# A list kernel for a two-layer graph network: one gather table per group instead of one for all, the last group's lists in buffers of their own, a changed planner, and ScalarE taking part in layer 1's sorting while layer 0 runs

## The chip, the cores and the metric

The kernel runs on one core of a Trainium2 chip. The metric is the device time of one execution in microseconds (us); the kernel before takes 1524.7 us in the median of three runs (1523.92 to 1529.08). The engines are called by the profile's names: PE (matrix products), DVE (VectorE), ACT (ScalarE), POOL (GpSimd) and SP, whose queue issues most plain DMAs. POOL issues the indirect DMAs (gathers and scatters whose rows are named by an index per partition).

## The reference

There are 16 graphs of 1024 nodes with 64 channels; `adj` (16 x 1024 x 1024, float32, 64 MB) holds edge weights and is sparse: a graph's first node is expected to have some 60 neighbours, most nodes fewer than 10.

```python
# layer 0
h = jnp.maximum(_layernorm(x), 0.0)
x = x + matmul(adj / clip(sum(adj, 2), 1), h)
# layer 1
h = jnp.maximum(_layernorm(x), 0.0)
adj_d = _dilate_adj(adj, mask)                       # drops every skip-th neighbour of long lists
agg = _weighted_nanquantile_agg(h, adj_d > 0)        # per channel: 0.25, 0.5 and 0.75 quantiles
out = h + agg                                        # over a node's neighbours, weights .25 .5 .25
y = relu(out @ W1 + b1) @ W2 + b2
x = x + y * mask
```

A quantile over the neighbours needs each node's neighbour rows sorted, channel by channel. That is the costly part.

## The kernel before, in words

The work is one program with two layers that overlap.

**Layer 0** goes batch by batch (one graph is a batch). SP loads eight adjacency row tiles of 128 x 1024 (`at`, 512 KB each, five buffers; `loads`). ACT makes signs of them with row sums (`sg`, `signs`); DVE multiplies the signs by a key and takes the eight largest of each of four segments (`rec`, the neighbour list of each node; `listing`, L598). PE transposes each tile into `pt` and ACT copies that to `att` (`transposes`, `turned`, L628); PE multiplies `att` with the normed `h` (`products`, L659); DVE adds the residual into `row`. `channels` (L704) norms the result, and SP writes it as 66 values a node to a DRAM table, `tab`, of which each batch has 1025 rows (the last holds "no neighbour"). `endings` (L716) puts the batch's nodes in order of their degree class: ACT writes the lists into `row`, DVE works out each node's place (`to`), and POOL sends the rows to `srt[g]` by eight scatters `srt<-row,to`.

**Layer 1** goes by groups of four batches. `group(g)` (L1069) starts when its four batches are done and, from the third group on, when all ten jobs of group g - 2 are done; it loads `recs` from `srt[g]`, takes the neighbours' numbers out of the lists (`keys`), makes row numbers (`idx`, `nodes_i`), and enters into the table which neighbours the dilation drops, by two scatters `tab<-drop,didx` (L1166). It then makes ten jobs, one for each cap on the list length (15, 10, 8, and so on down to 1; the nodes in order of length lie in 32 tiles of 128, tile 0 holds those of the long lists, and tiles of one cap make one job). `recs`, `keys`, `idx` and `nodes_i` have two buffers for four groups.

A `Job` (L800) asks for one gather per place of its lists: `places<-tab,idx` brings 128 rows of 66 values to 128 partitions (496 gathers over the kernel). `Job.sort` (L850) works out on DVE which neighbours are dropped (`rem`, `gone`, `ok`) and the quantile weights (`w`), masks dropped values with a huge number, runs a sorting network of minima and maxima on DVE between `places` and `other`, and multiplies the sorted values by the weights. The mask and the products can be done by ACT, one instruction of 128 x 64 for each place ("helped", L882 and L965: `places<-places,gone` and `prod<-places,w`), or by DVE, one or a few instructions for all of it. In the kernel before ACT does so once all 16 batches of layer 0 are done. `layers` (L1007) sums on PE (`pt<-ident,prod`), runs the MLP over ACT and PE, DVE makes `y`, and POOL scatters it to the output (`out_dram<-y,nodes_i`).

**The long lists.** `long_lists` (L1188) serves the 32 longest nodes of each graph, eight of each per list: four lists of 88, 31, 24 and 20 gathers. For each it gathers the nodes' adjacency rows (`lat`), takes the neighbours by repeated maxima, and makes a job with `lplaces0` (the list of 88, one buffer) or `lplaces` (the others, two buffers, L1269). These read the table of all 16 batches; DVE's first step of such a sort is `lrem<-lplaces,lS`, its weights are `lw`. It is added after layer 0, in a pool of its own that takes the room of layer 0's buffers, so its first DVE instruction (`rev`) stands behind them.

**The order.** DVE's and POOL's orders are written into the program (`manual_schedule`, L357); the other engines' follow the Tile scheduler. What writes them is `Plan` (L232). Each piece of work is a generator that yields the engine of its next step and the time from which that step can begin; `run` takes the step that can begin first, ties by rank. `note` keeps a clock per engine with costs for every operation, the time `ready` of each tile, and the time `used`. The clocks are the planner's own, and only set the order. The run takes the groups first (rank -2000), then layer 0's streams in the ranks at L1278 to L1283, then `long_lists`.

All recorded operations have the line L226, that of the helper that notes them.

Of the kernel before, what the change touches and what calls it, by code (L numbers as in the profile page):

```python
# [9 lines left out]
F32 = mybir.dt.float32  # L10
BF = mybir.dt.bfloat16
# [16 lines left out]
GB = 4  # L28
SUB = 32
# [4 lines left out]

CAPS = (
    [0, 15, 10, 8, 7, 7, 6] + [5] * 4 + [4] * 4 + [3] * 6 + [2] * 6 + [1] * 5
)
LONG = (88, 31, 24, 20)
# [193 lines left out]
class Plan:  # L232
# [4 lines left out]
    def __init__(self, nc):  # L237
# [7 lines left out]
        self.last = self.own = None  # L245

# [21 lines left out]
    def note(self, engine, op, args, kwargs):  # L268
# [12 lines left out]
        after = 0.15  # L281
        if engine == "DVE":
# [9 lines left out]
        elif engine == "POOL":  # L292
            time, after = (1.27, 2.2) if op == "indirect_dma_start" else (0.15, 0.1)
            self.last = None
        else:
            start = max(start, self.clock["DMA"])
            rate = 165e3 if 4 * out.shape[-1] >= 512 else 85e3
            time, after = 0.05, 2.2 + math.prod(out.shape) * 4 / rate
            self.clock["DMA"] = start + after - 2.2
        self.clock[engine] = end = start + time  # L300
        self.ready[out.tensor.name] = end + after
# [64 lines left out]
def list_path(ctx, tc, x, adj, nodemask, w1, b1, w2, b2, out, go):  # L366
# [7 lines left out]
    NG = B // GB  # L374
# [7 lines left out]
    NTAU = N // SUB  # L382
# [45 lines left out]
    which = consts.tile([P, 2], I32, name="which")  # L428
    nc.vector.tensor_scalar(which[:, 1:2], part, 3, None, op0=OP.logical_shift_right)
    nc.vector.tensor_scalar(which[:, 0:1], which[:, 1:2], GB - 1, None, op0=OP.bitwise_and)  # L430
    toff = consts.tile([P, 2], F32, name="toff")
    nc.vector.tensor_scalar(toff, which, float(TS), None, op0=OP.mult)
    noff = consts.tile([P, 2], F32, name="noff")
    nc.vector.tensor_scalar(noff, which, float(N), None, op0=OP.mult)
    caps = consts.tile([P, NTAU], F32, name="caps")
    for t, cap in enumerate(CAPS):
        nc.vector.memset(caps[:, t:t + 1], float(cap if t else N))
# [28 lines left out]
    tab = dram.tile([B * TS, W], F32, name="tab")  # L466
    srt = [dram.tile([GB * N, RW], F32, name=f"srt{g}") for g in range(NG)]
# [3 lines left out]
    nc.sync.dma_start(tab.rearrange("(b t) w -> b t w", t=TS)[:, N, :], none)  # L471
    pairs = tab.rearrange("r (a two) -> (r a) two", two=2)
# [5 lines left out]
    plan = Plan(nc)  # L478
    nc = plan.nc
# [224 lines left out]
    def channels(pool, now):  # L704

        for b, st in enumerate(batch):
# [3 lines left out]
            yield from normed(row()[:, :, :C], row()[:, :, X1:R0])  # L710
            nc.sync.dma_start(
                tab[b * TS:b * TS + N, :].rearrange("(t p) w -> p t w", p=P), row()[:, :, :W]
# [3 lines left out]
    def endings(pool, now):  # L716

        first = lambda rank: rank - 3000
        for b, st in enumerate(batch):
            now[0] = b  # L720
            g, gb = divmod(b, GB)
# [20 lines left out]
            for s in STEPS[1:]:  # L742
# [26 lines left out]
            nc.vector.tensor_scalar(low, low, LSUB - 1, None, op0=OP.bitwise_and)  # L769
            nc.vector.tensor_scalar(  # L770
                pos, pos, float(GB), float(LSUB * gb), op0=OP.mult, op1=OP.add
            )
            to = new(pool, [P, NT], I32, "to", 2)
            nc.vector.scalar_tensor_tensor(to, low, float(1 - GB), pos, op0=OP.mult, op1=OP.add)
# [26 lines left out]
    class Job:  # L801
# [3 lines left out]
        def __init__(self, pool, n, T, keys, idx, node, mask, nodes_i, table, S, g, name="places",  # L805
                     bufs=4, rank=0):
# [3 lines left out]
        def run(self):  # L810
# [6 lines left out]
                at(self.idx), room(self.name, self.bufs), room("S", 4) if short else 0.0  # L817
# [8 lines left out]
            for t in range(T):  # L826
                for k in range(n - 1):
                    if t or k:
                        yield "POOL", pace, *own
                    since.append(since[0] if since else plan.clock["POOL"])  # L830
                    gather(A[:, k + 1, t, :], self.table, self.idx[:, t, k:k + 1])
                    progress["ahead"] -= 1
# [17 lines left out]
        def sort(self):  # L850
# [31 lines left out]
            helped = progress["batches"] == B  # L882
# [82 lines left out]
            helped = progress["batches"] == B  # L965
# [41 lines left out]
        def layers(self, terms, sources):  # L1007
# [55 lines left out]
            for t in range(T):  # L1063
                yield "POOL", lambda: at(y) + LATE
                scatter(out_rows, y[:, t, :], self.nodes_i[:, t:t + 1], scatters)
# [3 lines left out]
    def group(g):  # L1069


        yield "SP", lambda: 0.0 if progress["batches"] >= (g + 1) * GB and (
            g < 2 or progress["jobs"][g - 2] == len(set(CAPS[1:]))
        ) else INF
        R = (g + 1) * GB
        table = tab[:R * TS, :]
        recs = new(grp, [P, NTAU, REC], F32, "recs", 2)
# [8 lines left out]
            nodes, node, noff[:, 0:1], float(g * GB * N), op0=OP.add, op1=OP.add  # L1086
        )
        nodes_i = new(grp, [P, NTAU], I32, "nodes_i", 2)
# [491 lines left out]
```

## Time and profile before

| | |
|---|---|
| median of three runs | 1524.7 us |
| profiled execution, its own time | 1525.97 us |
| its span | 1523.8 us |
| mean granted PE clock | 0.689 |
| DVE busy | 1211.9 us, 80% |
| POOL busy | 960.8 us, 63% |
| ACT busy | 752.9 us, 49% |
| PE busy | 751.5 us, 49% |
| last `to` of layer 0 (DVE) ends | 772.1 us |
| last `srt` scatter (POOL) ends | 791.8 us |
| first step of the first long list's sort (DVE) | 1087.6 us |
| last output scatter starts | 1515.2 us |

Busy time is the time of the instructions themselves. The time in which an engine issues a DMA or waits for a semaphore isn't in it; "idle" lines of a group say what ended that time ("issue" where nothing shown did). A group's line gives operation, output <- inputs, form, count | busy time, mean of one in ns | idle time just before them and what ended most of it. The windows view gives busy time and number of instructions of each engine between two moments.

### The profile page before, as it was taken

Reading aid. Unit: us, or ns where it says so; the run is one execution under the profiler, and the core shown is the slowest. Engines: PE = TensorE matmul, PEld = TensorE weight load, DVE = VectorE, ACT = ScalarE, POOL = GpSimd, SP = SyncE. Lnnn points to the kernel's source line nnn. Section 1 sums busy time; section 2 is a strip of 40 time slices with the busy share of each in tenths; the row PEclk is TensorE's granted clock in tenths of the full one; section 3 lists DMA queues with packets and bytes.
Section 4 is the critical chain, followed back from the end, with each engine's and each line's share of the span. In section 5 each row is a group of like instructions: output and inputs, shape, how many; then the busy total and the mean of one; then the engine's idle time right before and its main releaser. Section 6 shows DMA issues by size and latency. Waiting matters only on the chain. (4 is left out here: it accounts for less than half of the span.)

```text
span 1523.8 us, 15747 instructions
## 1 busy us (share of the span) xinstructions
PE 751.5 (49%) x3192; PEld 469.3 (31%) x3192; DVE 1211.9 (80%) x4119; ACT 752.9 (49%) x2503; POOL 960.8 (63%) x1156
## 2 busy tenths in 40 slices
PE   4887776576348777655825420013000056706454
PEld 2443342344214453432413320012000034605343
DVE  6878798999997699999734779995189999998852
ACT  7989878476436665675515320011410147516442
POOL 0122237745567766556677776567777777777774
PEclk8889987787568778767865655555555556857666
DMA  4555764455514354643322131221111111112110
GB/s 153 172 163 156 185 187 116 131 134 172 113 40 104 114 144 129 161 131 83 87 52 37 29 78 34 50 41 31 33 23 24 26 27 30 37 30 45 36 27 17
DMA packets 135536, 129.01 MB, mean 85 GB/s; under 512 B 100696, under 2 KB 103384, under 8 KB 135432
## 3 DMA queue, kind: packets, MB, share of 16 engines
q1 hardware_dynamic: 102696, 86.46, 20.6%
q0 software_dynamic: 32736, 41.47, 12.6%
q14 instruction: 76, 0.62, 0.1%
q8 instruction: 28, 0.46, 0.1%
HBM read 108.57 MB, written 19.28 MB: 84 GB/s over the span
## 5 line engine op out<-in xcount | busy, mean ns | idle before, releaser
L226 POOL DMA_INDIRECT places<-tab,idx x496 | 495.0, 998 | 161.2 <-issue 142.3
L226 PE MATMUL pt<-ident,prod 128*128 128x128 f32 (+1 forms) x736 | 159.1, 376 | 454.0 <-DVE prod L226 369.6
L226 PEld LDWEIGHTS pt<-ident,prod 128*128 128x128 f32 (+1 forms) x736 | 129.4, 257 | 486.1 <-ACT prod L226 287.8
L226 PE MATMUL ps_small<-att,h 128*65 128x512 f32 x512 | 255.4, 649 | 26.9 <-ACT h L226 22.4
L226 POOL DMA_INDIRECT srt<-row,to x128 | 129.6, 1013 | 208.8 <-ACT row L226 186.7
L226 PE MATMUL pt<-ident,at 128*128 128x128 f32 x1024 | 181.0, 324 | 106.7 <-ACT att L226 79.2
L226 POOL DMA_INDIRECT lplaces<-tab,lidx x163 | 166.9, 1024 | 53.7 <-issue 49.1
L226 PEld LDWEIGHTS pt<-ident,at 128*128 128x128 f32 x1024 | 138.5, 166 | 154.2 <-ACT att L226 104.8
L226 DVE MAX8 rec<-sg 128x8 f16<-128x256 f16 x512 | 180.1, 414 | 4.4
L226 ACT ACTIVATE sg<-at 128x1024 f16<-128x1024 f32 x128 | 135.1, 1056 | 69.4 <-DMA at<-in_adj_dram 48.8
L226 ACT COPY att<-pt 128x512 f32<-128x512 f32 x256 | 141.4, 583 | 28.4 <-PE pt L226 27.3
L226 POOL DMA_INDIRECT out_dram<-y,nodes_i x124 | 121.8, 983 | 37.9 <-issue 20.0
L226 PEld LDWEIGHTS ps_small<-att,h 128*65 128x65 f32 x512 | 75.7, 153 | 166.8 <-issue 127.6
L226 ACT ACTIVATE gone<-gone 128x18 f32<-128x18 f32 (+9 forms) x23 | 4.8, 208 | 234.1 <-DVE ok L226 234.1
L226 DVE TENSOR_TENSOR sg<-sg,keyed 128x1024 f16<-128x1024 f16 x128 | 87.4, 683 | 30.4 <-ACT sg L226 30.4
L226 DVE TENSOR_TENSOR long_other<-lplaces 128x512 f32<-128x512 f32 (+5 forms) x124 | 63.8, 557 | 21.8 <-ACT lplaces L226 21.6
L226 PE MATMUL ps_small<-ot,w_sb 128*128 128x128 f32 (+3 forms) x112 | 53.1, 564 | 53.3 <-ACT ot L226 22.5
L226 ACT COPY ot<-pt 128x128 f32<-128x128 f32 (+3 forms) x56 | 22.2, 396 | 109.6 <-PE pt L226 109.3
L226 DVE TENSOR_TENSOR other<-places,other 128x64 f32<-128x64 f32 (+6 forms) x204 | 69.6, 341 | 5.9
L226 ACT ACTIVATE places<-places,gone 128x64 f32<-128x64 f32 x283 | 70.7, 335 | 0.4
L226 ACT ACTIVATE prod<-places,w 128x64 f32<-128x64 f32 x157 | 39.5, 335 | 63.1 <-DVE w L226 63.1
L226 DVE TENSOR_TENSOR places<-places,other 128x64 f32<-128x64 f32 (+2 forms) x208 | 62.4, 310 | 4.9
(210 smaller groups left out, 1643.3 us busy)
## 6 DMA issues: line engine op xcount, KB each, us to landing
at<-in_adj_dram SPq DMA_DIRECT2D x128, 512.0 KB
places<-tab,idx POOLq DMA_INDIRECT x496, 2.5
tab<-row SPq DMA_DIRECT2D x16, 264.0 KB
xt<-in_x_dram SPq DMA_DIRECT2D x16, 256.0 KB
lplaces<-tab,lidx POOLq DMA_INDIRECT x163, 2.5
recs<-srt SPq DMA_DIRECT2D x4, 544.0 KB
srt<-row,to POOLq DMA_INDIRECT x128, 2.7
out_dram<-y,nodes_i POOLq DMA_INDIRECT x124, 2.2
```

The lines of the kernel that those rows point to most:

```text
L226: ins = getattr(self._engine, op)(*args, **kwargs)
```

## The change

In the size of group that is used (four, in `GROUPS`) the following changes. The parts for groups of two batches (`CAPS2`, `half`, `aside`) are not reached.

- `tab` becomes four tables `tabs[g]`, one per group. After a group's drop scatters SP copies its table into `whole` (DRAM to DRAM, 1.08 MB for each group). The short jobs gather from `tabs[g]`, the long lists from `whole`.
- The two drop scatters of a group are declared independent of each other, with a POOL memset between them.
- The last group has `recs`, `nodes_i`, `keys` and `idx` in buffers of their own ("last_"), doesn't wait for the jobs of the second group, and is added to the plan after layer 0, in the long lists' pool.
- `Plan`: SP's writes to `tabs` neither wait for nor move the table's `ready` time; a gather isn't planned later for the table's `ready` time (`own`), but the jobs begin after the drop (`begin`); a DMA's busy time in the planner's clock is its bytes by one rate.
- "helped" holds wherever the planner's clock of ACT stands less than 2.0 after that of DVE, in layer 0 too.

```diff
@@ -25,16 +25,18 @@
 
 QUANTILES = ((0.25, 0.25), (0.75, 0.25), (0.5, 0.5))
 
-GB = 4
-SUB = 32
+GROUPS = (4, 4, 4, 4)
 NSEG = 4
 STEPS = (16, 20, 24, 32)
 CLS = 15 + len(STEPS) + 1
 
 
+
+
 CAPS = (
     [0, 15, 10, 8, 7, 7, 6] + [5] * 4 + [4] * 4 + [3] * 6 + [2] * 6 + [1] * 5
 )
+CAPS2 = [CAPS[1]] + CAPS[2::2]
 LONG = (88, 31, 24, 20)
 LSEG = 8
 LCAPS = (24, 16, 16, 16)
@@ -243,6 +245,7 @@
         self.ready, self.used, self.users = {}, {}, {}
         self.slots, self.streams = {}, []
         self.last = self.own = None
+        self.parts = set()
 
     def tile(self, pool, shape, dtype, name, bufs, users=0):
 
@@ -279,6 +282,9 @@
             self.used.get(out.tensor.name, 0.0) if self.own is None else 0.0,
         )
         after = 0.15
+        apart = engine == "SP" and out.tensor.name in self.parts
+        if apart:
+            start = max(self.clock[engine], *(self.ready[v.tensor.name] for v in rest))
         if engine == "DVE":
             half = op == "tensor_tensor" and all(v.dtype == HF for v in (out, *rest))
             time = 0.04 if op == "memset" else 0.07 + size * (0.57e-3 if half else 1.04e-3)
@@ -294,11 +300,13 @@
             self.last = None
         else:
             start = max(start, self.clock["DMA"])
-            rate = 165e3 if 4 * out.shape[-1] >= 512 else 85e3
-            time, after = 0.05, 2.2 + math.prod(out.shape) * 4 / rate
-            self.clock["DMA"] = start + after - 2.2
+            busy = math.prod(out.shape) * 4 / 165e3
+
+            time, after = 0.05, 2.2 + busy * (1 if 4 * out.shape[-1] >= 512 else 2)
+            self.clock["DMA"] = start + busy
         self.clock[engine] = end = start + time
-        self.ready[out.tensor.name] = end + after
+        if not apart:
+            self.ready[out.tensor.name] = end + after
         for v in rest:
             self.used[v.tensor.name] = max(self.used.get(v.tensor.name, 0.0), end + after)
         if "accum_out" in kwargs:
@@ -463,19 +479,22 @@
 
 
 
-    tab = dram.tile([B * TS, W], F32, name="tab")
-    srt = [dram.tile([GB * N, RW], F32, name=f"srt{g}") for g in range(NG)]
+
+    tabs = [dram.tile([n * TS, W], F32, name=f"tab{g}") for g, n in enumerate(GROUPS)]
+    whole = dram.tile([B * TS, W], F32, name="whole")
+    srt = [dram.tile([GROUPS[g] * N, RW], F32, name=f"srt{g}") for g in range(NG)]
     none = consts.tile([B, W], F32, name="none")
     nc.vector.memset(none[:, :C], HUGE)
     nc.vector.memset(none[:, C:], -1.0)
-    nc.sync.dma_start(tab.rearrange("(b t) w -> b t w", t=TS)[:, N, :], none)
-    pairs = tab.rearrange("r (a two) -> (r a) two", two=2)
+    for tab, n in zip(tabs, GROUPS):
+        nc.sync.dma_start(tab.rearrange("(b t) w -> b t w", t=TS)[:, N, :], none[:n])
     adj_rows = adj.rearrange("b i j -> (b i) j")
     out_rows = out.rearrange("b n c -> (b n) c")
 
     scatters = []
     sorts = [[] for _ in range(NG)]
     plan = Plan(nc)
+    plan.parts.update(tab.tensor.name for tab in tabs)
     nc = plan.nc
     new, free, room, at = plan.tile, plan.release, plan.room, plan.at
     always = lambda: 0.0
@@ -708,8 +727,10 @@
             row = lambda: st["row"]
             yield "DVE", lambda: known(st, "row") if st["residual"] == 2 else INF
             yield from normed(row()[:, :, :C], row()[:, :, X1:R0])
+            g = max(g for g in range(NG) if FIRST[g] <= b)
+            lo = (b - FIRST[g]) * TS
             nc.sync.dma_start(
-                tab[b * TS:b * TS + N, :].rearrange("(t p) w -> p t w", p=P), row()[:, :, :W]
+                tabs[g][lo:lo + N, :].rearrange("(t p) w -> p t w", p=P), row()[:, :, :W]
             )
             st["normed"] = True
 
@@ -814,7 +844,7 @@
             own = () if short else (lambda rank: self.rank,)
             pace = lambda: since[0] + 1.3 * len(since) if not short else 0.0
             yield "POOL", lambda: max(
-                at(self.idx), room(self.name, self.bufs), room("S", 4) if short else 0.0
+                self.begin, at(self.idx), room(self.name, self.bufs), room("S", 4) if short else 0.0
             ), *own
             A = self.A = new(pool, [P, n, T, W], F32, self.name, self.bufs, users=1)
             progress["ahead"] += T * (n - 1)
@@ -828,7 +858,9 @@
                     if t or k:
                         yield "POOL", pace, *own
                     since.append(since[0] if since else plan.clock["POOL"])
+                    plan.own = plan.clock["POOL"]
                     gather(A[:, k + 1, t, :], self.table, self.idx[:, t, k:k + 1])
+                    plan.own = None
                     progress["ahead"] -= 1
             yield "DVE", lambda: max(
                 at(A, self.S) + SLACK,
@@ -879,7 +911,7 @@
                 q.unsqueeze(2).to_broadcast([P, K, count, T]), OP.subtract,
             )
 
-            helped = progress["batches"] == B
+            helped = plan.clock["ACT"] < plan.clock["DVE"] + 2.0
             if helped:
                 yield "ACT", lambda: at(gone) + SLACK
                 nc.scalar.mul(gone, gone, HUGE)
@@ -962,7 +994,7 @@
                 if count + 1 < total:
                     nc.vector.memset(prod[:, :, count + 1:, :], 0.0)
 
-            helped = progress["batches"] == B
+            helped = plan.clock["ACT"] < plan.clock["DVE"] + 2.0
             for copy in (1, 0):
                 mine = [k for k in range(count) if copies[k] == copy]
                 if helped and (copy == 0 or not short):
@@ -1062,19 +1094,25 @@
...
-    def group(g):
-
-
-        yield "SP", lambda: 0.0 if progress["batches"] >= (g + 1) * GB and (
-            g < 2 or progress["jobs"][g - 2] == len(set(CAPS[1:]))
+    def group(g, kept=grp, name=""):
+
+        size = GROUPS[g]
+        four = size == 4
+        caps, caps_sb, s = (CAPS, caps4, 0) if four else (CAPS2, caps2, 2)
+        NTAU = len(caps)
+        begin = 1 if four else 0
+        R = FIRST[g] + size
+
+        yield "SP", lambda: 0.0 if progress["batches"] >= R and (
+            g < 2 or name or progress["jobs"][g - 2] == len(set(CAPS[1:] if GROUPS[g - 2] == 4 else CAPS2))
         ) else INF
-        R = (g + 1) * GB
-        table = tab[:R * TS, :]
-        recs = new(grp, [P, NTAU, REC], F32, "recs", 2)
+        table = tabs[g]
+        recs = new(kept, [P, NTAU, REC], F32, name + "recs", 1 if name else 2)
         tiles = srt[g].rearrange("(t p) w -> p t w", p=P)
         nc.sync.dma_start(recs, tiles[:, :, R0:])
         yield "DVE", lambda: at(recs)
@@ -1083,9 +1121,9 @@
         mask = recs[:, :, REC - 1]
         nodes = new(grp, [P, NTAU], F32, "nodes", 1)
         nc.vector.tensor_scalar(
-            nodes, node, noff[:, 0:1], float(g * GB * N), op0=OP.add, op1=OP.add
-        )
-        nodes_i = new(grp, [P, NTAU], I32, "nodes_i", 2)
+            nodes, node, noff[:, s:s + 1], float(FIRST[g] * N), op0=OP.add, op1=OP.add
+        )
+        nodes_i = new(kept, [P, NTAU], I32, name + "nodes_i", 1 if name else 2)
         nc.vector.tensor_copy(nodes_i, nodes)
         progress["begun"] = g + 1
         yield "POOL", lambda: at(nodes_i)
@@ -1101,26 +1140,25 @@
...
-        base = tiny.tile([P, 1], F32, name="gbase")
-        nc.vector.tensor_scalar(base, toff[:, 0:1], float(g * GB * TS), None, op0=OP.add)
+        base = toff[:, s:s + 1]
         basep = tiny.tile([P, 1], F32, name="gbasep")
         nc.vector.tensor_scalar(basep, base, float(PW), float(C // 2), op0=OP.mult, op1=OP.add)
         based = tiny.tile([P, 1], F32, name="gbased")
         nc.vector.tensor_scalar(based, base, float(N), None, op0=OP.add)
 
         drop = new(tiny, [P, 2, 2], F32, "drop", 2)
-        keys = new(grp, [P, NTAU, 16], F32, "keys", 2)
+        keys = new(kept, [P, NTAU, 16], F32, name + "keys", 1 if name else 2)
         nc.vector.memset(keys, 0.0)
         left = tiny.tile([P, 8 * NSEG], F32, name="left")
-        for t in range(1, NTAU):
+        for t in range(begin, NTAU):
             nc.vector.max(out=keys[:, t, :8], in_=lists[:, t, :])
-            if CAPS[t] > 8:
+            if caps[t] > 8:
                 nc.vector.match_replace(
                     out=left, in_to_replace=keys[:, t, :8], in_values=lists[:, t, :],
                     imm_value=0.0,
@@ -1129,23 +1167,27 @@
...
         didx = new(tiny, [P, 2], I32, "didx", 2)
         index_of(didx, node[:, 0:2], float(PW), basep)
-        idx = new(grp, [P, NTAU, 16], I32, "idx", 2)
+        idx = new(kept, [P, NTAU, 16], I32, name + "idx", 1 if name else 2)
         index_of(idx, keys, -1.0, based)
@@ -1163,24 +1205,33 @@
                 accum_out=drop[:, 0, e:e + 1],
             )
         yield "POOL", lambda: at(drop)
-        for e in range(2):
-            nc.gpsimd.indirect_dma_start(
-                out=pairs[:R * TS * PW, :],
+        for e in range(2 if four else 1):
+            if e:
+                nc.gpsimd.memset(turn, 0.0)
+            ins = nc.gpsimd.indirect_dma_start(
+                out=table.rearrange("r (a two) -> (r a) two", two=2),
                 out_offset=bass.IndirectOffsetOnAxis(ap=didx[:, e:e + 1], axis=0),
                 in_=drop[:, e, :], in_offset=None,
             )
+            if e:
+                tc.declare_no_dep(ins.ins, other, reason="rows of their own")
+            other = ins.ins
+        dropped = at(table)
+        yield "SP", lambda: dropped
+        nc.sync.dma_start(whole[FIRST[g] * TS:R * TS, :], table)
         classes = []
-        for t in range(1, NTAU):
-            if classes and CAPS[t] == CAPS[classes[-1][0]]:
+        for t in range(begin, NTAU):
+            if classes and caps[t] == caps[classes[-1][0]]:
                 classes[-1].append(t)
             else:
                 classes.append([t])
         for i, ts in enumerate(classes):
-            n, T = CAPS[ts[0]] + 1, len(ts)
+            n, T = caps[ts[0]] + 1, len(ts)
             sl = slice(ts[0], ts[-1] + 1)
             job = Job(
                 gat, n, T, keys[:, sl, :n - 1], idx[:, sl, :], node[:, sl], mask[:, sl],
                 nodes_i[:, sl], table, tiles[:, sl, :R0], g,
+                half=0 in ts, begin=dropped,
             )
             plan.add(job.run(), 100 * g + i)
         progress["groups"] = g + 1
@@ -1265,13 +1317,13 @@
 
             yield "DVE", lambda: 0.0 if progress["groups"] == NG else INF
             job = Job(
-                pool, n, 1, keys, idx.unsqueeze(1), node, mask, nodes_i, tab, S, NG,
-                *(("lplaces", 2) if l else ("lplaces0", 1)), -600 + l,
+                pool, n, 1, keys, idx.unsqueeze(1), node, mask, nodes_i, whole, S, NG,
+                *(("lplaces", 2) if l else ("lplaces0", 1)), -600 + l, begin=at(whole),
             )
             plan.add(job.run(), 100 * NG + l)
 
     progress = {"batches": 0, "begun": 0, "groups": 0, "ahead": 0, "jobs": [0] * (NG + 1)}
-    for g in range(NG):
+    for g in range(NG - 1):
         plan.add(group(g), -2000)
     with tc.tile_pool(name="lay0", bufs=2) as pool:
 
@@ -1283,6 +1335,8 @@
             plan.add(stream(pool, now), lambda first=first, now=now: 10 * now[0] + first)
         plan.run(lambda: progress["batches"] == B)
     with tc.tile_pool(name="long", bufs=1) as pool:
+
+        plan.add(group(NG - 1, pool, "last_"), -2000)
         plan.add(long_lists(pool), -1500)
         plan.run()
     nc = tc.nc
```

## The prediction

> **What bounds the kernel now.** I read first the page's table of engines and its costliest groups, then the busy time by stage, then the waits, then single lines of the timeline where a stage turns. The chain of waits on the page ends at once (it follows the last register work), so it does not guide here.
>
> ```profile
> PE 751.5 (49%) x3192; PEld 469.3 (31%) x3192; DVE 1211.9 (80%) x4119; ACT 752.9 (49%) x2503; POOL 960.8 (63%) x1156
> L226 POOL DMA_INDIRECT places<-tab,idx x496 | 495.0, 998 | 161.2 <-issue 142.3
> L226 POOL DMA_INDIRECT lplaces<-tab,lidx x163 | 166.9, 1024 | 53.7 <-issue 49.1
> L226 POOL DMA_INDIRECT srt<-row,to x128 | 129.6, 1013 | 208.8 <-ACT row L226 186.7
> L226 ACT ACTIVATE places<-places,gone 128x64 f32<-128x64 f32 x283 | 70.7, 335 | 0.4
> ```
>
> VectorE is busiest, 1212 us of 1523.8. A gather holds Pool for 0.94 us and 0.30 us of issue, so 1.25 us each. The 931 indirect DMAs make Pool's real load some 1160 us, not 961. Two queues of about 1200 us that feed each other are the bound.
>
> ```profile
> 0.00:175.10 175.10, 128.72 (x520) 68.87 (x521) 130.34 (x447) 154.38 (x476) 36.72 (x72) 0.88 0.53 159
> 175.10:791.80 616.70, 399.26 (x1651) 229.72 (x1649) 530.74 (x1800) 369.44 (x1123) 387.06 (x487) 0.77 0.46 123
> 791.80:1087.60 295.80, 67.13 (x262) 50.09 (x262) 197.84 (x717) 57.24 (x221) 210.99 (x237) 0.54 0.21 42
> 1087.60:1515.30 427.70, 156.38 (x760) 120.58 (x760) 352.98 (x1156) 171.89 (x684) 325.15 (x363) 0.60 0.16 30
> ```
>
> The rows (length, then PE, PEld, DVE, ACT, POOL busy) are: start; layer 0 with the first lists; from the last `srt` scatter to the first long list's sort; the rest. Layer 0 ends late (772 us on VectorE), and then two stages hold VectorE at 67% and 83%.
>
> ```profile
> POOL srt L226 <- ACT row L226: 186.7, 24, 64.7
> DVE rev L226 <- DMA srt<-row,to: 15.1, 1, 15.1
> POOL lat L226 <- DVE lnodes_i L226: 16.8, 3, 8.0
> DVE other L226 <- ACT places L226: 23.6, 6, 6.5
> POOL tab L226 <- DMA tab<-drop,didx: 7.7, 4, 3.0
> ```
>
> Those were waits (total us, times, longest). From the timeline (start, us, idle before it and what ended that):
>
> ```profile
> 1087.59 0.34 DVE L226 TENSOR_TENSOR lrem<-lplaces,lS 128x176 f32<-128x176 f32 x1 [29.23 <-DMA lplaces<-tab,lidx]
> 1393.07 0.94 POOL L226 DMA_INDIRECT lplaces<-tab,lidx  x1 [4.31 <-PE pt L226]
> 1515.21 0.96 POOL L226 DMA_INDIRECT out_dram<-y,nodes_i  x1 [0.19 <-POOLq L360]
> ```
>
> Pool stands for 187 us in layer 0, for rows that ScalarE finishes late. VectorE waits 15.1 us at the stage's turn and 29 us for the first long list's 88 gathers. The last long list's gathers (1393) wait until PE frees the buffer of the second list, and the last scatter goes out at 1515.2; 8.6 us after its start the span ends.
>
> **What the Trainium skill says.** (1) "DMA: Bandwidth & Descriptors", "Anatomy of one DMA — SWDGE (gpsimd) path": about 2.0 us fixed per such DMA. The trace agrees: 1.7 us pass from the end of the 88th gather to `lrem`. (2) The same page, "Two DMAs through the same engine are not ordered": a DMA that reads what another wrote must wait for its completion semaphore. So each `whole` copy waits for the landing of its group's drop scatters; the 7.7 us over 4 above are such waits. (3) "ScalarE: Activation LUTs", "What ACT_TABLE_LOAD costs": an ACTIVATE with a pointer operand takes 280 ns + 0.833 ns per element, and back-to-back ones overlap by 93 ns; for 64 elements 333 and 240 ns. The trace has 335, one every 240 to 250 ns: agrees. (4) "Why a DMA increments its semaphore by 16 and not by 1" of the first page prices the copy, below.
>
> **The change part by part.** VectorE's and Pool's orders are written into the program, so I set the two programs' orders side by side and summed, in each engine's order, the trace's duration plus issue pause for each operation and shape. A position in these sums is no time; real time minus position I call lag. Before, VectorE's whole queue is 1239 us, after 1219; Pool's is 1160 and 1159. Up to the end of layer 0 (`to` of batch 15; last `srt` scatter):
>
>     engine   before   after   real time before   lag before
>     DVE      686      749     772.1              86
>     POOL     506      651     791.8              285
>     ACT      494      601     751.5              257
>
> The new planner brings list work forward: 117 more Pool DMAs lie ahead of the last `srt` scatter. What follows has so much less to do. VectorE's total falls by 20 us, since 17 masks of some 0.9 us (15.6 us) and products (6.8 to 2.3 us) go to ScalarE, which gets 213 masks and 56 products more at 0.25 us: +68 us in all, +107 ahead of layer 0's end (the rest moved from behind it). ScalarE waits 254 us in the first 800, which is the cover.
>
> *End of layer 0.* Before, VectorE's lag went 37 (batch 3), 51 (batch 7), 73 (position 455 to 623), 86. Pool's position was 43 in both orders at 175 (`srt` of batch 3), so it must now do 651 - 43 = 608 us between 175 and this end. Taking the tightest crossings by position: Pool's drop of group 2 (476.5) needs VectorE's 597.4, so its lag is at least 73 + 121 = 194, +2 for sync; VectorE's position 649.5 needs Pool's gathers to 537.4, with 2 us to landing: 537.4 + 196 + 2 - 649.5 = 86, 13 over the 73 of before. With the 8 that the last batch adds, 94 to 96. Crossings with ScalarE come back to within 3 to 5 us of each other (ScalarE's 532.6 needs VectorE's 618.0, and VectorE's 691.3 needs ScalarE's 598.4): I add 4. Lag 100, from 86 (it stays) to 142 (below). `to` at 749 + 100 = 849.
>
> *The copies.* Nothing in the trace copies DRAM to DRAM. Below: 1.08 MB in 30 rows on 15 engines of the skill's 27 GiB/s, an estimate of 2.5 us + 2 fixed. Above: the profile page's 155 to 187 GB/s of the loads, 6 to 7 us + 2. I take the upper; it lies beside the other work. Three stand on SP's queue ahead of adjacency loads (issued only 4 to 7 us before use in most batches), which then wait for the drop's landing, 2 to 3 us: 0 to 10 us each at worst, counted in the range and in the 4. The last is done at about 909, and its first reader, a gather of the first long list, is due at 930 to 940: nothing on the path.
>
> *Drop scatters, last group's buffers.* The second drop no longer waits: 7.7 us of Pool's, at places where Pool waits for VectorE anyway; I take 0. Before, `nodes_i` of the last group started at 905.5, after the jobs of group 1; now it follows the turn: the `srt` start 4 after `to`, eight scatters 9.9, one output scatter 1.2, landing 2, SP 1.2, and 10.2 from the `recs` load's issue to `nodes_i` (178.8 to 189.0): 28.5, so 877.5. That is the 15.1 us wait in its new place.
>
> *First long list.* From there 102.5 us of VectorE to the third list's `lnodes` (762.6 to 865.1): 980.5 with 0.5 sync. Then 73 Pool DMAs, 92.4 us (one after another, since they are ready), 1 of drift, 1.7 landing: `lrem` at 1075.6 instead of 1087.6. VectorE has 31 us to do in these 95, so some 65 us stand idle: most of what was brought forward is spent here.
>
> *To the second list.* 276 us of VectorE up to list 1's weights (895.7 to 1171.6), before 284 real. I add 44: 16.1 us of handoffs to ScalarE (3.62 + 4 x 3.12) and gaps of the dependent sort 11, both from the same stretch of before, sync 6, and 11 where Pool's position plus landing comes after VectorE's (1139.9). 1395.5. Before: 1372.0; so this stage is later, since VectorE had more left in after's order between the lists.
>
> *Last list.* PE needs 12 us to free the buffer (1407.5; before 21, since PE began on it 14 us late), 20 gathers 25 + 1.7 (1434), sort 27.3 (before 26.6), sums and MLP 12 (1473.5; 1457.4 to 1472.3 before, with 5 us of order), scatter and end 0.3 + 8.6: span 1482.4. The profiled execution was 1525.97 for 1523.8, so +2.2; it stands 1.3 over the median of the runs: 1482.4 + 2.2 - 1.3 = 1483.3. Predicted: 1483 us, 2.7% less.
>
> **The rivals.** *ScalarE becomes layer 0's bound (slower).* Its queue is in order, and its signs, copies of transposes and rows now stand behind masks that wait for gathers. For: 187 us of Pool's idle time already await its rows. From batch 3 to 15 it had 373 us of work in 609, 236 of stops. If these stay, the row of batch 15 comes at 142.8 + 479.6 + 236 = 858 and `to` 21 later, 879; each of 25 helped jobs then adds the tail's wait of VectorE for masks (23.6 us for 23 jobs, so 1.0 each; 0 to 6.5): 905, 56 over 849, and the end 1539. It decides from a slip of 42 on. Against: most of the 236 are waits for VectorE and PE, which extra work fills.
>
> *Pool's stops stay (no change).* In 175 to 792 Pool has 154 us without work. My 849 leaves 863 - 175 - 608 = 80. If 121 are left, the end comes 41 later, 1524.
>
> *The waits go (faster still).* Lag stays 86 (-14), and of the 44 only the 16 and 11 remain (-17): 1452.
>
> **Chances.** Forecast 0.53, still faster 0.17, no change 0.10, slower 0.20. I put the forecast's own tail at about 15 us on each side, and some of the slower case's below 1532. Range 1450 to 1532: about 1 in 10 outside above, 1 below. A measurement of this kernel tells 0.3% (4.6 us) from no change. Faster 0.70, same 0.09, slower 0.21.
>
> **What would show it.** Right: `to` of batch 15 at about 849, later than the 772 of before; `lrem` near 1076 with a wait of VectorE for `lplaces` of 60 us or more; the last list's first gather near 1408, behind PE; ScalarE's masks at 496 in number, half in layer 0. Wrong: layer 0 ending beyond 890, with VectorE waiting for ScalarE's `sg` or `places`, or with loads behind a copy; gathers of `whole` that wait for its copy; Pool's idle time before 863 over 120 us.

## The result, and the profile after

The changed kernel takes 1513.6 us in the median of four runs (1512.82 to 1514.1), the kernel before 1525.0 beside it: a ratio of 0.992, with a 95% interval of 0.990 to 0.994. The forecast was 1483, with a range from 1450 to 1532. So the direction was right, and a quarter of the size came: 11 us of the 42 forecast. Nine of the runs told of below belong to sets in which every kernel, the one before too, took 30% longer; each is compared only with the kernels that ran beside it.

The profile's lines for the changed kernel, in the order in which those of before were shown; first engines and groups from the page (the profiled execution has a span of 1511.0 us and a time of 1512.82):

```profile
PE 738.8 (49%) x3192; PEld 464.7 (31%) x3192; DVE 1191.3 (79%) x4104; ACT 816.4 (54%) x2789; POOL 957.2 (63%) x1154
L228 POOL DMA_INDIRECT places<-tab,idx x372 | 370.2, 995 | 131.7 <-issue 101.8
L228 POOL DMA_INDIRECT srt<-row,to x128 | 125.9, 984 | 165.8 <-ACT row L228 144.0
L228 ACT ACTIVATE places<-places,gone 128x64 f32<-128x64 f32 x496 | 123.5, 335 | 0.5
```

VectorE is busy 20.6 us less and ScalarE 63.5 more. The masks stand at 496 of 335 ns, as counted from the order. But VectorE's 20.6 us became 12.8 of the span. The windows, cut at the same turns of the work as those of before (the start, up to 178.3 us, is left out; layer 0 with lists, up to the last `srt` scatter; up to the first long list's sort; the rest; columns as there):

```profile
178.30:889.20 710.90, 453.57 (x1897) 275.32 (x1896) 593.92 (x2079) 494.90 (x1663) 501.21 (x620) 0.76 0.43 118
889.20:1096.50 207.30, 31.98 (x124) 21.58 (x123) 127.22 (x445) 21.33 (x76) 153.20 (x172) 0.53 0.21 51
1096.50:1502.10 405.60, 124.98 (x668) 100.62 (x668) 336.49 (x1106) 145.44 (x579) 264.93 (x291) 0.60 0.12 26
```

Layer 0's window has grown from 617 to 711 us. VectorE's share in it was 86% and is 84%, although it now has 63 us more to do there. The third stage shrank from 296 to 207. Single lines of the timeline (start, us, and the idle time before it with what ended it):

```profile
870.31 0.20 DVE L228 SCALAR_TENSOR_TENSOR to<-low,pos 128x8 int32<-128x8 int32 x1
1096.53 0.34 DVE L228 TENSOR_TENSOR lrem<-lplaces,lS 128x176 f32<-128x176 f32 x1 [48.89 <-DMA lplaces<-whole,lidx]
1434.22 0.97 POOL L228 DMA_INDIRECT lplaces<-whole,lidx  x1 [6.22 <-PE pt L228]
1502.09 0.96 POOL L228 DMA_INDIRECT out_dram<-y,lnodes_i  x1 [1.73 <-DVE bad L1346]
```

Each is later than forecast: 870.5 for 849, 1096.5 for 1075.6, 1434.2 for 1407.5, and the last scatter 1502.1 for 1473.8. The 21 us are there at the end of layer 0, and go through to the end.

VectorE's waits over 0.15 us add up to 40 us in layer 0 (175 to 772) before, and 72 (175 to 870) after; behind it to 155 before and 137 after. So the change took 18 us of waiting out of the list stages and put 32 into layer 0. These are the waits of layer 0 (total us, times, longest), before:

```profile
DVE sg L226 <- ACT sg L226: 12.2, 7, 4.4
DVE deg L226 <- PE ps_small L226: 9.1, 4, 3.5
DVE rem L226 <- DMA places<-tab,idx: 6.1, 2, 5.8
```

and after:

```profile
DVE rem L228 <- DMA places<-tab,idx: 15.4, 6, 4.9
DVE other L228 <- ACT places L228: 14.2, 7, 4.8
DVE sg L228 <- ACT sg L228: 14.0, 4, 8.7
DVE base L228 <- PE ps_small L228: 10.7, 3, 6.5
DVE prod L228 <- PE pt L228: 7.3, 1, 7.3
```

`other<-places`, the first step of a sort, waits for ScalarE's masks (`places`): a wait that layer 0 did not have before. `base` and `prod` wait for PE. The forecast had half of the 496 masks in layer 0; ahead of the last `to` stand 301 of them. This is the longest of the seven waits:

```profile
360.45 0.19 DVE L228 SCALAR_TENSOR_TENSOR ok<-keys,gone 128x20 f32<-128x20 f32 x1
361.82 4.88 ACT L228 ACTIVATE places<-places,gone 128x64 f32<-128x64 f32 x20
366.25 0.43 DVE L228 TENSOR_TENSOR other<-places 128x256 f32<-128x256 f32 x1 [4.84 <-ACT places L228]
```

ScalarE begins the masks 1.2 us after VectorE's `ok` is done, and VectorE stands for nearly the whole of their run.

### The profile page after: what moved, and what is told of

Its sections match the earlier page's. It is cut to its first block, busy times and chain, and to the rows that moved or that the text cites. A ratio compares the mean times of both kernels' runs of the same rounds, so it can differ in the third digit from the quotient of the medians.

```text
span 1511.0 us, 15983 instructions
## 1 busy us (share of the span) xinstructions
PE 738.8 (49%) x3192; PEld 464.7 (31%) x3192; DVE 1191.3 (79%) x4104; ACT 816.4 (54%) x2789; POOL 957.2 (63%) x1154
## 5 line engine op out<-in xcount | busy, mean ns | idle before, releaser
L228 POOL DMA_INDIRECT places<-tab,idx x372 | 370.2, 995 | 131.7 <-issue 101.8
L228 POOL DMA_INDIRECT srt<-row,to x128 | 125.9, 984 | 165.8 <-ACT row L228 144.0
L228 PE MATMUL pt<-ident,at 128*128 128x128 f32 x1024 | 176.7, 320 | 96.0 <-ACT att L228 71.1
L228 POOL DMA_INDIRECT lplaces<-whole,lidx x163 | 167.2, 1026 | 55.6 <-issue 48.5
L228 POOL DMA_INDIRECT places<-tab,last_idx x124 | 123.8, 998 | 41.3 <-issue 35.0
L228 ACT ACTIVATE places<-places,gone 128x64 f32<-128x64 f32 x496 | 123.5, 335 | 0.5
L228 ACT ACTIVATE prod<-places,w 128x64 f32<-128x64 f32 x213 | 54.1, 336 | 120.5 <-DVE w L228 120.5
L228 POOL DMA_INDIRECT out_dram<-y,nodes_i x93 | 91.8, 987 | 22.6 <-issue 15.1
L228 ACT ACTIVATE gone<-gone 128x15 f32<-128x15 f32 (+9 forms) x40 | 8.2, 206 | 169.2 <-DVE ok L228 169.0
L228 PE MATMUL ps_small<-ot,w_sb 128*128 128x128 f32 (+3 forms) x112 | 47.6, 513 | 44.2 <-DVE y L228 31.2
```

The costliest lines, as they stand in the source:

```text
L228: ins = getattr(self._engine, op)(*args, **kwargs)
```

## The experiments

Two theories for the 21 us. A: ScalarE's masks in layer 0 hold up VectorE, directly and through everything behind them in ScalarE's order. B: adjacency loads are held back in SP's queue. For B speaks this stretch of SP's timeline in the changed kernel:

```profile
493.51 0.35 SPq L228 DMA_DIRECT2D at<-in_adj_dram  x1
496.98 0.38 SPq L228 DMA_DIRECT2D tab<-row  x1
530.18 0.38 SPq L228 DMA_DIRECT2D y<-srt  x1
530.66 0.41 SPq L228 DMA_DIRECT2D at<-in_adj_dram  x1
```

For 33 us SP stands at the residual load `y<-srt` of a short job, whose `y` buffer waits for an older job's output scatters, and the adjacency loads stand behind it. ScalarE then waits 24.5 us for its next tile:

```profile
534.31 1.06 ACT L228 ACTIVATE sg<-at 128x1024 f16<-128x1024 f32 x1 [24.50 <-DMA at<-in_adj_dram]
```

**1. Without ScalarE's help in layer 0.**

```diff
-            helped = plan.clock["ACT"] < plan.clock["DVE"] + 2.0
+            helped = progress["batches"] == B
```

> The changed kernel with ScalarE's masks and products only after layer 0 (780 us of VectorE's queue up to the last `to`, 471 after it). Theory A: lag 95 to 103, `to` at about 880, the time about 1523. Theory B: lag 117 to 123, `to` at about 899, the time about 1542.

1532.7 us (ratio 1.0041, 1.0027 to 1.0055). The last `to` ends at 876.1, a lag of 96 over its 780: inside what A gave. The time, halfway between A's 1523 and B's 1542, does not tell them apart: the rest of the profiled run took 651 us instead of 640, with VectorE's waits there at 147 for 137, and that run (1528.7) was one of the shorter. So in layer 0 the changed kernel, with the help, has 25 us more lag than this order without it, and 31 less in VectorE's queue up to that point.

**2. ScalarE's help alone, in the kernel before** (the same line, the other way).

> The kernel before with only ScalarE's help in layer 0 added (683 us of VectorE's queue up to the last `to`, 537 after). Theory A: VectorE waits 14 us for masks there, `to` at about 783, the time about 1520. Theory B: `to` at about 769, the time about 1506. A third reading, since the slower chip had it 2% over the kernel before: ScalarE's masks hold up its signs and transposes, `to` over 800 and the time over 1530.

1534.2 us (1.0053, 1.0035 to 1.0071): slower than before, the third reading. `to` ended at 826 though VectorE's queue up to it was 683: a lag of 143. VectorE's waits in layer 0 were 94 us, of which

```profile
DVE other L226 <- ACT places L226: 30.1, 8, 6.7
DVE deg L226 <- PE ps_small L226: 16.5, 7, 5.8
DVE base L226 <- PE ps_small L226: 15.0, 3, 9.2
```

are the largest. Here 20 helped jobs with 62 us of masks came with 57 us more lag (143 for 86), more than twice what 25 jobs cost in the changed kernel. Why the order of the planner before lets them cost so much more was not tried.

**3. The last group's own buffers.** Out of the changed kernel, and alone in the kernel before:

```diff
-    for g in range(NG - 1):
+    for g in range(NG):
         plan.add(group(g), -2000)
...
-        plan.add(group(NG - 1, pool, "last_"), -2000)
```

> The changed kernel with the last group's lists in the shared buffers again, added with the other groups and waiting for the jobs of group 1. VectorE's and Pool's orders come out the same as in the changed kernel, since by then the planner has finished group 1. If the own buffers matter in the changed kernel (its rival: they don't, since group 1's jobs are done when layer 0 ends): `nodes_i` of the last group later than 26 us after the last `to` and the time more than 5 us over the changed kernel's. If they don't: within 3 us of it.

> The kernel before with only the last group's own buffers added. If the wait of the last group was worth something: `lrem` near 1031 and the time 1505 to 1515. If VectorE's idle time only moves: 1521 to 1526. Over 1530, as on the slower chip: the order that comes out of it is worse at the end, with the last lists' output behind other gathers.

Out of the changed kernel: 1511.1 in one run, `nodes_i` of the last group 25.8 us after the last `to` (26.0 in the changed kernel). No effect of the buffers is seen there; both engines' orders are the same without them. Alone in the kernel before: 1559.8 us (1.0231, 1.0214 to 1.0248), over 1530 as in the last of its expectations. `lrem` came at 1020, even sooner than the 1031 hoped for, but the last scatter at 1548. VectorE's waits behind layer 0 were 192 us for 155:

```profile
DVE lrem L226 <- DMA lplaces<-tab,lidx: 43.5, 1, 43.5
DVE rem L226 <- DMA places<-tab,last_idx: 30.4, 5, 8.9
DVE lat L226 <- DMA lat<-in_adj_dram,lnodes_i: 18.2, 3, 14.2
```

With the long lists this early, VectorE has to wait for the last group's own gathers, which come later. The last long list's sort still began 12 us sooner than in the kernel before (1418.9 for 1430.8); the time is lost behind it, where Pool had 60 gathers of short jobs left to issue, for 30 before.

**4. More `y` buffers.** Ten physical buffers; the planner keeps counting six.

```diff
-            y = new(mlp, [P, T, CO], F32, "y", 6, users=1)
+            y = mlp.tile([P, T, CO], F32, name="y" if T > 2 else "y_few", bufs=5)
+            plan.slots.setdefault("y", []).append(y.tensor.name)
+            plan.users[y.tensor.name] = 1
```

> Ten physical buffers for `y`, VectorE's and Pool's orders those of the changed kernel, now that the kernel before is near 1525 us again. Theory B (loads held back in SP's queue): ScalarE's waits for adjacency tiles fall from 66 us to about 30, the last `to` ends 10 to 20 us before the changed kernel's 870, the time is 1494 to 1504. Theory A (ScalarE's share of the sorts made the lag): `to` and the time within 3 us of the changed kernel's (1510 to 1517).

1515.0 us (0.9938, 0.9917 to 0.9958), no different from the changed kernel; but the wait was still there, with another job's load at its head, so this did not test B:

```profile
535.42 1.06 ACT L228 ACTIVATE sg<-at 128x1024 f16<-128x1024 f32 x1 [24.00 <-DMA at<-in_adj_dram]
```

**5. Masks and residual loads left out, in the unchanged order.** Neither VectorE's nor Pool's order changes, since the planner still notes what isn't issued. The first edit below leaves out the masks, the second the residual loads:

```diff
-                        nc.scalar.activation(val, val, AF.Identity, bias=gone[:, k - 1, t:t + 1])
+                        if progress["batches"] == B:
+                            nc.scalar.activation(val, val, AF.Identity, bias=gone[:, k - 1, t:t + 1])
+                        else:
+                            plan.note("ACT", "activation", (val, val, AF.Identity),
+                                      {"bias": gone[:, k - 1, t:t + 1]})
...
-                nc.sync.dma_start(x1, self.residual)
+                plan.note("SP", "dma_start", (x1, self.residual), {})
```

> The changed kernel without ScalarE's 321 mask instructions of layer 0 (dropped neighbours stay unmasked there), with VectorE's and Pool's orders exactly those of the changed kernel. Theory A: these 77 us of ScalarE make the lag that the forecast missed; VectorE's lag at the last `to` falls from 121 to 96 to 102, `to` at 845 to 851, the time about 1490. Theory B: it stays within 5 us (865 or more), the time 1508 or more.

> The changed kernel without the residual loads `y<-srt` of the short jobs (their output lacks the residual: DVE adds a constant tile in its place), with VectorE's and Pool's orders exactly those of the changed kernel. Ten `y` buffers had left the 24 us wait at 535 in place, so this takes the loads away instead. Theory B (they hold back the adjacency loads in SP's queue): ScalarE's waits for adjacency tiles under 35 us (66), the last `to` 10 to 20 us before 870, the time 1495 to 1505. Theory A: `to` and the time within 4 us of the changed kernel's (1510 to 1517).

> Both left out, masks of layer 0 and residual loads. If each costs its own time: the two gains add. If both stand for the same wait (ScalarE's signs come late either way): no more than the larger of the two, within 4 us.

Without the masks: 1492.1 us (0.9772, 0.9756 to 0.9788), 21.5 less than the changed kernel (the two medians stand in different sets; the spans of the two profiled runs differ by 20.6). These lines of its timeline stand at the forecast's own numbers, 849 and 1075.6:

```profile
849.46 0.19 DVE L228 SCALAR_TENSOR_TENSOR to<-low,pos 128x8 int32<-128x8 int32 x1
1075.68 0.34 DVE L228 TENSOR_TENSOR lrem<-lplaces,lS 128x176 f32<-128x176 f32 x1 [51.88 <-DMA lplaces<-whole,lidx]
```

Without the residual loads: 1507.4 us (0.9861, 0.9836 to 0.9886), some 6 less than the changed kernel; `to` at 866.6. ScalarE's waits for adjacency tiles went from 66 to 41 us and the one of 24.5 is gone, but `to` came only 4 us sooner. Without both: 1492.3 us, no better than without the masks. So A made the 21 us; what the residual loads cost is not added to it. The 6 us alone lie between the two expectations; B as stated, 10 to 20 us, falls. ScalarE's 140 products ahead of the last `to` were left in; what they cost was not tried.

**6. Three buffers for the long lists 1 to 3.**

```diff
-                *(("lplaces", 2) if l else ("lplaces0", 1)), -600 + l, begin=at(whole),
+                *(("lplaces", 3) if l else ("lplaces0", 1)), -600 + l, begin=at(whole),
```

> The changed kernel with three buffers for the long lists 1 to 3 in place of two, so that the last list's 20 gathers need not wait until PE frees the first one (the forecast's step ahead of the last list). If that wait is on the path: 1495 to 1503. If VectorE's queue sets the end there (it is idle only 1.2 us before the last list's sort): 1508 to 1515.

1522.3 us (0.9964, 0.9948 to 0.998): 9 us more than the changed kernel, outside both expectations. The last list's gathers now go at 1180 instead of 1434, and its sort no longer waits for them at all:

```profile
1467.89 0.19 DVE L228 TENSOR_TENSOR lrem<-lplaces,lS 128x40 f32<-128x40 f32 x1
```

It starts right behind list 2's weights, at 1467.9 where the changed kernel has 1462.7. But in this profiled run, at 1525.8 the longest of its eight, the last `to` was already 6.9 us later (877.4), whose cause is open. Counted from the last `to`, the sort begins 1.7 us sooner, and what follows it takes 56.2 us for 48.3. The run does not isolate the wait: with a third buffer the planner also makes other orders (Pool's differ from 1172.8 us on, and ScalarE has 236 products for 213). So the wait for PE was worth little at that place, where VectorE in the changed kernel stood idle for it 1.2 us; which of the other differences costs the 8 us behind it is open.

**7. On the slower chip.**

Experiments 1 to 4 had been run there first, in two sets, with expectations in the times of the other chip. The expectations speak of a slower chip; that the chip is the cause isn't shown. For each run the ratio to the kernel before beside it follows. The first set:

> The changed kernel, with ScalarE's masks and products only after layer 0 again, as before. By its order VectorE has 780 us of work up to the last `to` (749 in the changed kernel, whose lag there was 121) and 471 after it (470). Theory A, ScalarE's share of the sorts in layer 0 made the lag: VectorE's waits for masks (14 us) and most of those behind them go, the lag is 95 to 103, `to` ends at about 880 and the time is 880 + 643 = 1523. Theory B, loads held back in SP's queue made it: the lag stays 117 to 123, `to` at about 899, the time is 1542.

1.0101 (1.0069 to 1.0133).

> The changed kernel with ten physical buffers for `y` (five for jobs of up to two tiles, five for the others) in place of six; the planner still counts six, so VectorE's and Pool's orders are those of the changed kernel and only SP's residual loads `y<-srt` need not wait for an output scatter. Theory B: ScalarE's waits for adjacency tiles fall from 66 us to about 30, those of 24.5 and 10.1 us go, the last `to` ends 10 to 20 us earlier (about 855) and the time is about 1498. Theory A: `to` and the time move by less than 3 us (1511 to 1514).

0.9897 (0.9856 to 0.9938).

> The kernel before with ScalarE helping in layer 0 as in the changed kernel, and nothing else of the change. VectorE has 683 us of work up to the last `to` (686 before) and 537 after it (553). Theory A: VectorE waits some 14 us for masks there, `to` at about 783 and the time about 783 + 737 = 1520, hardly faster. Theory B: no such wait, `to` at about 769, 1506.

1.0201 (1.0148 to 1.0255).

> The kernel before with the last group's lists in buffers of their own, added after layer 0, and nothing else of the change. Layer 0's order is that of before: `to` at 772. The first long list's sort stands at 844 in VectorE's queue instead of 900. If the wait of the last group was worth something: `lrem` near 1031 and the time 1505 to 1515. If VectorE's idle time only moves to a later place: 1521 to 1526.

1.0175 (1.0122 to 1.0228).

The second set, with the changed kernel as a base:

> The changed kernel once more, as the base for the other runs of this call, since the call before had every kernel about 30% slower. As first measured: 0.9925 of the kernel before (1513.6 us against 1525); on a chip with longer stalls of all engines the ratio may be anything from 0.97 to 1.02.

0.9924 (0.9903 to 0.9946), the same ratio as on the other chip.

> Ten physical buffers for `y` again, VectorE's and Pool's orders those of the changed kernel. Theory B (loads held back in SP's queue): 10 to 20 us less than the changed kernel of this call, the waits of ScalarE for adjacency tiles halved. Theory A (ScalarE's share of the sorts): within 3 us of it.

0.9944 (0.9919 to 0.9969).

> The changed kernel with ScalarE's masks and products only after layer 0. Theory A: lag at the last `to` 95 to 103, that is `to` at about 880 and the time some 10 us over the changed kernel's. Theory B: lag 117 to 123, `to` at about 899, the time about 28 us over the changed kernel's.

1.0067 (1.0033 to 1.01).

> The kernel before with only ScalarE's help in layer 0 added. Theory A: `to` at about 783, the time some 5 us under the kernel before. Theory B: `to` at about 769, some 19 us under it.

1.019 (1.0148 to 1.0232).

The times of the first set fit no expectation, since these were in times of the other chip. In the second set the changed kernel's ratio lies in its wide range, and the `y` buffers came 2.1 us from it, as A had it. Without help in layer 0 the time was 27 us over the changed kernel's, as B had it; but the last `to` came only 4.1 us later (1158.4 for 1154.3), nearer to A's 10 than to B's 28. The kernel before with help came 39 us over the kernel before, where neither theory has it. Other stops are in all these times (last section), so only the signs are taken from them: they are those of the other chip. A last run there moved the residual load one step back in the program:

```diff
-            if self.short:
-                nc.sync.dma_start(x1, self.residual)
-            else:
+            if not self.short:
                 x1 = self.S[:, :, X1:R0]
...
                 free(pt)
+                if self.short and t0 == 0:
+                    nc.sync.dma_start(x1, self.residual)
```

> The changed kernel with each short job's residual load issued one step later in the program, after ScalarE's copy of the sums instead of ahead of PE's sums; VectorE's and Pool's orders are those of the changed kernel. If the residual loads that wait in SP's queue for an output scatter cost what leaving them out gained (some 4 to 6 us), a later place gives back a part: 1507 to 1511. If SP still reaches them ahead of that scatter: 1511 to 1516, no gain.

0.9909 (0.9883 to 0.9936), not to be told from the 0.9924 of the changed kernel there; open.

## Why the prediction was right or wrong

The step that failed is the end of layer 0: "Crossings with ScalarE come back to within 3 to 5 us of each other", for which it added 4, to a lag of 100. The lag was 121.5. I compared positions in the two queues, and found ScalarE never more than a few microseconds late. What this comparison leaves out is the handoff itself: VectorE releases a batch of masks, has little or nothing else in its order, and waits until they have run. In the two longest waits, 4.84 and 3.62 us, ScalarE began its 20 and 16 masks 1.2 and 0.4 us after VectorE's `ok`, and the masks themselves took 4.88 and 3.92 us. In the other five, 5.7 us together, it came to them later, between signs, transposes' copies and rows. Experiment 5 prices it: 321 masks at 0.24 us are 77 us of ScalarE, and they cost 20.9 us of lag (870.5 - 849.65) and 21.5 of the time, for the 4 that I had added. 14.2 us of it are seen as waits for masks; how the rest comes about isn't told apart. ScalarE's 254 us of idle time did not cover them. The rival named the mechanism (ScalarE's share of the sorts holds up layer 0); its size, 56 us, was too much in the changed kernel, since its first term, that all 236 us of ScalarE's stops stay, did not hold. The other rival, that Pool's stops stay, falls: Pool's waits of over 0.6 us between 175 us and the last `srt` scatter went from 135 to 79, and to 56 without the masks.

The forecast's other terms, each against what was measured:

- *Pool's and VectorE's crossings*: right within some 5 us. Without ScalarE's masks the lag was 100.6 (849.65 - 749) in the unchanged order, for the 94 to 96 forecast without ScalarE's 4; in the run with no help in layer 0, of another order, it was 96. That 849 came out to a microsecond is luck, since the 849 had ScalarE's masks in it.
- *Turn of the stage and first long list*, 226.6 us from `to` to `lrem`: measured 226.0. VectorE's wait there was 49 us, under the 60 that I had set as the sign; the rest of the idle time is in front of earlier steps.
- *To the second list*: 44 us of overhead forecast, 53 measured (1425.4 - 1096.5 - 276). The handoffs were 16.9 for 16.1; the 11 us of waits for gathers did not come, and 13.6 us of waits for short jobs' masks (`other<-places`) and 5 for PE did: once more a wait for masks that had no term.
- *PE's release of the buffer*: 12 forecast, 8.8 measured. Treating it as the path was barely right: VectorE was idle only 1.2 us ahead of the last list's sort, and with the wait gone (experiment 6) that sort began only 1.7 us sooner after the last `to`.
- *Time over span*: +0.9 forecast, +2.6 for the median measured.

Sum: 21.5 (lag) - 0.6 + 9 - 3.2 + 1.9 (last sort to the end) + 1.7 = 30.3, the miss.

*Copies and SP's queue*: "0 to 10 us each at worst". SP waited 9.1 and 3.0 us for the drop scatters in layer 0, and ScalarE had no wait of over 3 us for a tile close behind either; the 21.5 us for the last group come behind the last adjacency load. (These are reads that wait for a write to land. The 7.7 us over 4 that the prediction set beside them were something else: the second drop scatter waiting for the first.) The gathers of `whole` never waited for their copy. What does hold back adjacency loads are the residual loads, which I had not looked at; leaving them out is worth some 6 us, with the masks in place.

*Last group's buffers*: I let the earlier `nodes_i` follow from them. It follows from the order: without them, in experiment 3, it came as early.

*What is left of the change*: neither of its large parts gains alone; each is slower than the kernel before. In rows the planner, tables and buffers, in columns where ScalarE helps (1525 and 1514 are the two kernels themselves):

    us                          help after layer 0    help in layer 0
    as before                        1525                 1534
    as changed                       1533                 1514

The new planner alone brings lists forward to where ScalarE did not help, so VectorE does more masks itself (its queue is 1251 us, 1239 before). With help it is 1219, 20 us less than before; 11 us of gain came of it.

## What to carry to other kernels

Work that is given to an engine with idle time isn't free when it is released by, and waited for by, the engine that is to be relieved: here 77 us of masks, in a stage where ScalarE had stood idle for 254 us, cost 21. Before crediting a stage's idle time as cover, look whether the relieved engine already waits like that ("`other` <- ACT `places`" here) in a stage where the work is shared, and charge for it: 1.0 us a job in the tail of before times 25 jobs would have been 25, near the 21 measured. The prediction had this figure in a rival and not in its own sum. Take that as a first estimate and no more: in the kernel before, with other orders, 20 such jobs came with 57 us more lag. And a position in a summed queue tells which engine is ahead, but not what each handoff costs.

## What the runs showed of the hardware

A mask of 128x64 on ScalarE took 335 ns alone, and a row of 20 took 4.88 us, 0.24 us each.

In three sets of runs all kernels took 30% longer (1973 to 1997 us for the kernel before), with the same durations of masks, 335 ns, and gathers, 0.94 us in the median. PE's `pt<-ident,prod` took 396 ns in the mean for 377, with a mean granted clock of 0.64 for 0.70. What was added is for the most part idle time that the profile puts to "remote" and "issue", more of it on ScalarE (501 us in the changed kernel) than on VectorE (276). In the changed kernel of the second set (ScalarE's waits; total us, times, longest):

```profile
ACT ot L228 <- remote: 144.4, 9, 40.6
ACT att L228 <- remote: 94.9, 18, 24.9
ACT lplaces L228 <- issue: 61.0, 60, 1.8
```

In the faster runs the same kernel has no wait for "remote". What causes it is open, the part of the chip in it too.
